# One more empty part on the attention chain's way out, and shared-expert pieces left out beside every fourth part of the last chain

## The chip, the cores and the metric

The kernel runs on one NeuronCore of a Trainium2 chip (trn2). The metric is the device time of one execution in microseconds: 706.55 us is the median of three timed runs before the change (703.7 to 708.07). The engines are named as in the profile: PE (TensorE matmul), PEld (its weight loads), DVE (VectorE), ACT (ScalarE), POOL (GpSimd) and SP (SyncE, which issues most DMAs).

## The reference: what is computed

Two transformer layers over 4 sequences of 512 tokens with 128 features, each sublayer followed by a residual and a layernorm:

```
x = LN(x + banded_attention(x))      # 16 heads of 8, each token sees 64 to either side
x = LN(x + moe0(x))                  # shared GEGLU expert (256 wide) + top 2 of 12 GEGLU experts (384 wide)
x = LN(x + ssm(x))                   # state-space mixer, 4 heads of 64, sequence of 64 states
x = LN(x + moe1(x))                  # top 2 of 8 experts (512 wide), each with its own layernorm
```

The change touches the attention and the first MoE. There, with `g` the weights of the two chosen experts:

```
ys = geglu(x @ Ws1 + bs1) @ Ws2 + bs2                        # every token
yr = sum over chosen e of g[e] * (geglu(x @ We1[e] + be1[e]) @ We2[e] + be2[e])
x  = LN(x + ys + yr)
```

## The kernel before

**Attention.** `attention` runs a software pipeline over g = -5 to 33. A batch has 8 steps (four blocks of 128 keys, two halves of heads). Each turn of the loop writes, in this order: `attention_exp` of step g (scores `pse`, L808; exponentials on ACT, L812; band mask on POOL, L816), a slot; `attention_max_end` and `attention_max` of steps further ahead (band and scores `psc`, L771 and L778; row maxima on DVE, L784; `pmax`, L791; the update of `q`, L794), a slot; `attention_values` of step g - 2 (`pc`, L831, then at a batch's end the copy `sum`, L838), a slot. All of it is traced under `as_written`, which keeps each engine's instructions in the order of the program (only the scatters of one run may change places among themselves).

**Chains.** What follows a batch's attention is a chain of parts, a generator; each slot (`advance(1)`) runs one part. A chain starts at the last slot of g = 8b + 9, so that three run inside the loop and the fourth has one part there. In order the parts are, for one batch:

- `attention_out`: (1) POOL adds the bias to x (L844), DVE turns the sums and inverts (L849, L851); (2) DVE spreads the inverses (`wide`, L854), turns them (L856) and scales both sums (L859); (3) nothing; (4) the output projection on PE (`po`, L865); (5) DVE adds it to x (L870) and takes statistics (L323, L324); `layernorm`: (6) square root on ACT (L304); (7) reciprocal and offset on DVE (L306, L314); (8) ACT normalises (L317).
- `moe0_shared`: (9) nothing; (10) transposes and their copy (`tp_xt`, L295, L298); (11) nothing; (12) the router (`pl`, L958); `gates`: (13) the first maximum (L340 to L354); (14) the second, and a tanh on ACT (L368); (15) gate weights (L375 to L381); then `moe0_dense` of this batch is put on the list `later`; `route`: (16) `rh` on DVE (L419) and two POOL writes (L422, L425); (17) ranks on PE (`prank`, L430 to L439); (18) DVE works out the rows `put` (L445 to L459); (19) to (22) two scatters each on POOL (L472); for the last batch (23) `route_end`, which makes the table of tiles on DVE (L485 to L516).

**Shared experts.** `moe0_dense` has six pieces: (1) the gates' transposes `tp_gt` on PE and a memset on POOL (L977, L979); (2) the copy `gt` on ACT (L981), two matmuls `pg_s` (L986) and their GELU `ge_s` (L990); (3) two matmuls `pa_s` (L995); (4) `act_s` on DVE (L998); (5) the projection `pys` (L1005, L1007); (6) the add `y` on DVE (L1012). None runs inside the loop.

**Tail.** After the loop `attention` returns `tail()`, which gives out the fourth chain's remaining parts and puts one piece of `later` behind each. `tiles` then works through the 43 expert tiles (PE `pxs_a` L560, `pg` and `pa` L1028, `py_a` L580; loads on SP, L547 and L548; scatter on POOL). It cannot write the first load before the table of tiles exists (`while "rows" not in r: next(beside)`), so the tail runs up to `route_end` first; what is left of it is written beside the tiles, at a budget of 1.0 us a tile against the cost that each piece yields.

PSUM has one pool of six banks that `psc`, `pse`, `po`, `pmax`, `tp_xt`, `pl`, `pg_s`, `pa_s`, `pys` and the tiles take in turn: a bank is free again when its reader has read it.

Of the kernel before, what the change touches and what calls it, by code (L numbers as in the profile page):

```python
# [39 lines left out]
class Kernel:  # L40
# [57 lines left out]
    def behind(self, x, y):  # L98

        order = mybir.DependencyInfo(mybir.DependencyClass.NoSync, mybir.DependencyReason.DATA)  # L100
        self.tc.add_manual_dep(x.ins, y.ins.name, order, reason="as written")
# [738 lines left out]
    def attention_out(self, b, s):  # L840

        nc = self.nc
        xb = s["x"][..., :D]
        nc.gpsimd.tensor_tensor(xb, xb, self.bo[:, None, :].to_broadcast([P, NT, D]), ALU.add)  # L844

        inv = self.sm.tile([P, 16, 4], F32, tag="inv", name=f"inv{b}")
        for cp in range(2):
            turned = self.ctx.tile([P, 16, 32], F32, tag="turned", name=f"turned{b}_{cp}")
            nc.vector.transpose(turned.rearrange("p k r -> p (k r)"), s["sum", cp])  # L849
            at = 16 - 16 * cp  # L850
            nc.vector.reciprocal(inv[:, :, 2 * cp : 2 * cp + 2], turned[:, :, at : at + 16 : HD0])  # L851
        yield 2.1
        wide = self.ctx.tile([P, 16, 4, HD0], F32, tag="turned", name=f"wide{b}")
        nc.vector.tensor_copy(wide, inv[:, :, :, None].to_broadcast([P, 16, 4, HD0]))  # L854
        scale = self.ctx.tile([P, T], F32, tag="turned", name=f"scale{b}")
        nc.vector.transpose(scale, wide.rearrange("p k c d -> p (k c d)"))  # L856
        for cp in range(2):
            x = s["sum", cp]
            nc.vector.tensor_tensor(x, x, scale, ALU.mult)  # L859
        yield 2.5  # L860
        yield 0.0
        po = self.bank(f"po{b}")
        for i in range(NT):
            for cp in range(2):
                nc.tensor.matmul(  # L865
                    po[:, i * P : (i + 1) * P], lhsT=s["sum", cp][:, i * P : (i + 1) * P],
                    rhs=self.wo2[:, cp, :], start=cp == 0, stop=cp == 1,
                )
        yield 1.5
        nc.vector.tensor_tensor(xb, po.rearrange("p (i d) -> p i d", i=NT), xb, ALU.add)  # L870
        mv = self.small([P, NT, 2], "mv", 6)
        for i in range(NT):
            self.stats(xb[:, i, :], mv[:, i, :])
        yield 2.6
        yield from self.layernorm([xb[:, i, :] for i in range(NT)], mv)
        return s["x"]

    def attention(self, x, behind):

        self.attention_consts()
        steps = 2 * NT
        ahead, lag = 5, 2
        state = [{} for _ in range(NB)]
        chains, self.later = [], []

        def chain(b):
            y = yield from self.attention_out(b, state[b])  # L890
            yield from behind(b, y)

        def advance(n):
            for c in list(chains):
                for _ in range(n):
                    if next(c, None) is None:
                        chains.remove(c)
                        break

        for _ in self.attention_qk(0, x[0], state[0]):  # L900
            pass
        for g in range(-ahead, NB * steps + lag):
            b, u = divmod(g, steps)
            if 0 <= b < NB:
                self.attention_exp(b, u, state[b])
            if g == 0:
                chains.append(self.ssm_consts())
            advance(1)
            b, u = divmod(g + ahead - 1, steps)
            if u % 2 and 0 <= b < NB:  # L910
                self.attention_max_end(b, u // 2, state[b])
            b, u = divmod(g + ahead, steps)
            if b < NB:
                self.attention_max(b, u, state[b])
            advance(1)
            b, u = divmod(g - lag, steps)
            if 0 <= b < NB:
                self.attention_values(b, u, state[b])
                if u == steps - 1:
                    chains.append(chain(b))  # L920
            if g == -ahead:
                self.attention_weights()
            b, u = divmod(g + ahead + 4, steps)
            if 0 < b < NB and u < 3:
                if u == 0:
                    state[b]["qk"] = self.attention_qk(b, x[b], state[b])
                next(state[b]["qk"])
            b, u = divmod(g + steps - 3, steps)
            if u == 0 and b < NB:
                self.attention_v(b, state[b])  # L930
            advance(1)

        def tail():

            parts = (part for c in chains for part in c)
            for part in parts:
                yield part
                while self.later:
                    if next(self.later[0], None) is not None:
                        break  # L940
                    self.later.pop(0)
            for c in self.later:
                yield from c

        return tail()


# [856 lines left out]
```

## Time and profile before

| | us |
|---|---|
| median of three timed runs | 706.55 |
| their range | 703.7 to 708.07 |
| the profiled execution, device time | 697.46 |
| its span, first to last instruction | 695.8 |
| its busy time: PE | 511.5 |
| PEld | 374.2 |
| DVE | 417.3 |
| POOL | 357.3 |
| ACT | 313.4 |

The profile was taken of one execution with a mean granted TensorE clock of 0.83. A timeline line gives start, duration, engine, source line, operation, output and inputs, shape, count, and in brackets how long the engine had been idle before and what released it. In lines of busy time by stretches, the pairs after the comma are busy us and (number of instructions) of PE, PEld, DVE, ACT and POOL; the last three numbers are the granted clock, the DMA engines' share and GB/s. Line numbers are those of the kernel before; after the change those below L860 are one higher, and those below L937 four.

### The profile page before, as it was taken

The page shows a single profiled execution, that of the slowest core. Times are in us where ns is not written, and L with a number is a line of the kernel's source. Part 1 is how long each engine was busy: PE and PEld are TensorE (multiplying, and loading weights), DVE is VectorE, ACT ScalarE, POOL GpSimd, SP SyncE. Part 2 cuts the span into 40 slices and gives each one's busy share as a digit, 9 for nine tenths or more (in the row PEclk, how much of TensorE's full clock was granted, in tenths as well). Part 3 has the DMA queues.
Part 4 walks back from the last instruction along what each step waited for, and adds up shares of the span by engine and source line. Part 5 has one row for each costly group of instructions (what it writes and reads, how often), then busy time and mean ns, then how long its engine had stood idle before and what let it go on. Part 6 is the DMA issues. An engine that isn't in the chain of part 4 may idle for free. (4 is left out here: it accounts for less than half of the span.)

```text
span 695.8 us, 13449 instructions
## 1 busy us (share of the span) xinstructions
PE 511.5 (74%) x4264; PEld 374.2 (54%) x4264; DVE 417.3 (60%) x1412; ACT 313.4 (45%) x816; POOL 357.3 (51%) x509
## 2 busy tenths in 40 slices
PE   6899788779977894999994474853675669899700
PEld 2344354254544553999994342622464469888700
DVE  5565656666734361466663359799784526777845
ACT  2154544443461511355552666934323317566525
POOL 8354323823747032355553217378773646888830
PEclk9899989979978695899998566977575559999955
DMA  6999999993000004488884402212110135666442
GB/s 171 244 162 164 165 165 162 166 163 51 32 2 32 0 16 152 126 254 251 239 255 148 144 0 78 76 48 76 46 48 19 44 112 168 167 181 170 121 130 61
DMA packets 93936, 83.63 MB, mean 120 GB/s; under 512 B 8869, under 2 KB 78650, under 8 KB 93866
## 3 DMA queue, kind: packets, MB, share of 16 engines
q1 hardware_dynamic: 88554, 71.85, 47.0%
q0 software_dynamic: 5312, 10.92, 5.2%
q8 instruction: 35, 0.57, 0.4%
q14 instruction: 35, 0.29, 0.1%
HBM read 50.54 MB, written 32.20 MB: 119 GB/s over the span
## 5 line engine op out<-in xcount | busy, mean ns | idle before, releaser
L816 POOL TENSOR_SCALAR_AFFINE_SELECT pt<-pt 128x1024 f32<-128x1024 f32 (+1 forms) x64 | 61.6, 987 | 95.4 <-ACT pt L812 89.1
L784 DVE TENSOR_REDUCE maxima<-psc 128x2 f32<-128x384 f32 x128 | 62.4, 549 | 45.3 <-PE psc L778 45.3
L812 ACT ACTIVATE pt<-pse 128x384 f32<-128x384 f32 (+1 forms) x128 | 59.2, 550 | 64.0 <-PE pse L808 64.0
L472 POOL DMA_INDIRECT ys_a<-io_a,at_a x43 | 42.1, 979 | 50.5 <-DVE at_a L571 37.9
L1037 DVE SCALAR_TENSOR_TENSOR act<-pa,bias_a,ge 128x128 f32<-128x128 f32 x129 | 37.4, 345 | 50.1 <-ACT ge L1036 29.1
L1631 ACT ACTIVATE hid<-ph,bias_b 128x128 f32<-128x128 f32 x156 | 44.6, 369 | 23.7 <-PE ph L1628 21.2
L771 PE MATMUL psc<-band,ident_bf 128*64 128x384 bf16 (+1 forms) x192 | 39.3, 351 | 12.6 <-ACT pt L812 7.5
L1036 ACT ACTIVATE ge<-pg,bias_a 128x128 f32<-128x128 f32 x129 | 38.1, 366 | 21.4 <-DVE at_a L571 17.7
L472 POOL DMA_INDIRECT table_a<-x,put x32 | 31.9, 996 | 24.6 <-issue 14.8
L1628 PE MATMUL ph<-io_b,wt_b 128*128 128x128 f32 x312 | 43.2, 283 | 0.0
L472 POOL DMA_INDIRECT ys_b<-io_b,at_b x39 | 39.1, 1002 | 7.4 <-issue 5.5
L808 PE MATMUL pse<-q,k 32*128 32x256 f32 (+1 forms) x512 | 41.1, 394 | 1.8 <-DVE q L794 1.8
L472 POOL DMA_INDIRECT table_b<-r,put x32 | 32.1, 1003 | 19.6 <-issue 7.9
L580 PE MATMUL py_b<-down,hid 128*128 x312 | 41.8, 277 | 0.3
L1628 PEld LDWEIGHTS ph<-io_b,wt_b 128*128 128x128 f32 x312 | 39.5, 199 | 0.0
L580 PEld LDWEIGHTS py_b<-down,hid 128*128 128x128 f32 x312 | 38.1, 192 | 1.2 <-issue 0.7
L1028 PE MATMUL pg<-io_a,wt_a 128*128 128x128 f32 x258 | 37.2, 282 | 0.0
L808 PEld LDWEIGHTS pse<-q,k 32*128 32x128 f32 x512 | 29.1, 198 | 15.0 <-issue 6.8
L1028 PE MATMUL pa<-io_a,wt_a 128*128 128x128 f32 x258 | 37.1, 282 | 0.0
L580 PE MATMUL py_a<-down,act 128*128 x258 | 35.8, 276 | 0.0
L831 PE MATMUL pc<-pt,v 128*32 128x256 f32 (+1 forms) x512 | 34.1, 390 | 0.6 <-POOL pt L816 0.6
L1028 PEld LDWEIGHTS pa<-io_a,wt_a 128*128 128x128 f32 x258 | 33.6, 199 | 0.0
(342 smaller groups left out, 1222.0 us busy)
## 6 DMA issues: line engine op xcount, KB each, us to landing
wt_a<-in_We_dram SPq DMA_DIRECT2D x43, 384.0 KB
table_a<-zero SPq DMA_DIRECT2D x12, 1040.0 KB
wt_b<-in_w_dram SPq DMA_DIRECT2D x39, 256.0 KB
table_b<-zero SPq DMA_DIRECT2D x8, 1040.0 KB
dbc<-rows SPq DMA_DIRECT2D x8, 512.0 KB
io_a<-table_a SPq DMA_DIRECT2D x43, 65.0 KB
io_b<-table_b SPq DMA_DIRECT2D x39, 65.0 KB
down<-in_We_dram SPq DMA_DIRECT2D x12, 192.0 KB
```

The lines of the kernel that those rows point to most:

```text
L472: put = self.nc.gpsimd.indirect_dma_start(out=out, out_offset=bass.IndirectOffsetOnAxis(ap=at, axis=0), in_=x, in_offset=None)
L580: nc.tensor.matmul(py[:, :D], lhsT=hidden[:, c * P : (c + 1) * P], rhs=flat[:, bass.ds(r["reg"][t, 2] + c * D, D)], start=c == 0, stop=c = ...
L771: nc.tensor.matmul(pp[part], lhsT=self.ident_bf[:, part], rhs=self.band[:, None, off : off + w].to_broadcast([P, 2, w]), start=True, stop= ...
L784: nc.vector.tensor_reduce(self.maxima[b % 2][:, j, at : at + 2], pp, AX.X, ALU.max)
L808: nc.tensor.matmul(pp[:, c], lhsT=s["k"][strip, 2 * cp + c, m * P : (m + 1) * P], rhs=s["q"][strip, c, lo:hi], start=True, stop=True, skip ...
L812: nc.scalar.activation(pt[:, 2 * i : 2 * i + 2, :w], pp, AF.Exp)
L816: nc.gpsimd.affine_select(out=x, in_=x, compare_op=ALU.is_ge, fill=0.0, base=HALF if m == 0 and sign > 0 else 0, pattern=[[0, 2 * G], [sig ...
L1028: nc.tensor.matmul(p[:, c * P : (c + 1) * P], lhsT=wt[:, at : at + P], rhs=xt, start=True, stop=True,)
L1036: nc.scalar.activation(ge[:, cb], pg[:, cb], AF.Gelu, bias=bias[:, 3 + c : 4 + c])
L1037: nc.vector.scalar_tensor_tensor(act[:, cb], pa[:, cb], bias[:, c : c + 1], ge[:, cb], ALU.add, ALU.mult)
L1628: nc.tensor.matmul(ph[:, cb], lhsT=s["wt"][:, cb], rhs=s["xt"], start=True, stop=True)
L1631: nc.scalar.activation(hid[:, cb], ph[:, cb], AF.Gelu, bias=s["bias"][:, c : c + 1])
```

## The change

In `attention_out` a second part without work stands between the scaling of the sums and the output projection, so that every later part of each chain comes one slot later. In `tail` the parts are counted from 0, and behind parts 3, 7, 11, 15 and 19 (and so on) no piece of the shared experts is written.

```diff
@@ attention_out
             x = s["sum", cp]
             nc.vector.tensor_tensor(x, x, scale, ALU.mult)
         yield 2.5
+        yield 0.0
         yield 0.0
         po = self.bank(f"po{b}")
@@ tail
             parts = (part for c in chains for part in c)
-            for part in parts:
+            for n, part in enumerate(parts):
                 yield part
+
+                if n % 4 == 3:
+                    continue
                 while self.later:
                     if next(self.later[0], None) is not None:
                         break
```

## Prediction

> **What bounds the kernel now.** The chain of work that ended last is traced back only to 485 us of the span, behind both edits, so I read the stages from busy time by stretches (columns: PE, weight loads, DVE, ACT, POOL busy us with counts, granted TensorE clock, DMA share, GB/s), then from each engine's timeline.
>
> ```profile
> 81.90:133.40 51.50, 43.26 (x488) 22.62 (x488) 31.90 (x93) 24.45 (x50) 21.77 (x24) 0.93 1.19 164
> ...
> 213.50:266.60 53.10, 40.18 (x172) 25.17 (x172) 22.76 (x71) 14.67 (x24) 20.52 (x28) 0.82 0.06 20
> ...
> 285.50:373.30 87.80, 87.74 (x786) 87.51 (x783) 57.01 (x253) 46.98 (x163) 48.17 (x81) 1.00 0.77 231
> ```
>
> First row: one batch's round of the attention loop. PE leads (43 of 51.5 us) and loses 8 us to waits. Second: the tail, where no engine is full; one dependent chain sets it. Third: the expert tiles, where PE has no gap at all: each matmul added there is paid in full. What follows waits for the tiles' results, so a shift up to 373 us reaches the end.
>
> PE's timeline shows where it stops:
>
> ```profile
> 86.57 3.81 PE L865 MATMUL po<-wo,sum 128*128 128x128 f32 x16 [2.53 <-DVE sum L859]
> ...
> 99.34 0.84 PE L771 MATMUL psc<-band,ident_bf 128*64 128x384 bf16 x4 [1.56 <-ACT pt L812]
> ...
> 273.40 0.79 PE L1005 MATMUL pys<-be,gt 13*128 13x128 f32 x2
> 275.16 1.45 PE L1007 MATMUL pys<-w_Ws,act_s 128*128 128x128 f32 x4 [0.97 <-DVE act_s L998]
> ```
>
> The output projection waits 2.53, 4.96 and 0.93 us in the three rounds inside the loop and then runs at the low clock (3.81, 3.87, 2.34 us). Just behind, PE waits for exponentials; ACT's timeline says why:
>
> ```profile
> 93.64 1.28 ACT L304 ACT_TABLE_LOAD   x1
> 94.93 0.30 ACT L304 ACTIVATE rstd<-mv,eps 128x4 f32<-128x4 f32 x1
> 97.40 1.28 ACT L812 ACT_TABLE_LOAD   x1 [2.17 <-PE pse L808]
> 98.69 2.06 ACT L812 ACTIVATE pt<-pse 128x512 f32<-128x512 f32 x4
> ```
>
> The layernorm's square root costs two table loads, and the next exponentials stand behind it. On DVE:
>
> ```profile
> 94.37 1.95 DVE L784 TENSOR_REDUCE maxima<-psc 128x2 f32<-128x384 f32 x4 [0.97 <-PE psc L778]
> ...
> 135.48 3.36 DVE L854 COPY wide<-inv 128x512 f32<-128x512 f32 x1
> ...
> 247.92 0.69 DVE L1012 TENSOR_TENSOR y<-pys,x 128x512 f32<-128x512 f32 x1 [2.57 <-PE pys L1007]
> ```
>
> Every step's four row maxima hold DVE for 1.95 us; what is written behind them waits.
>
> **The change, part by part.** No instruction is added or removed. The empty part moves each later part of a chain by one slot of the written order (after the exponentials, after the maxima, after the values). The skip takes pieces n = 3, 7, 11, 15, 19 out of the tail: 21 pieces ran before the routing table's end, 17 will.
>
> *First round in the loop.* The projection now stands behind the next step's scores (pse). Half of these have free banks and run at 84.0; the other half needs banks that the maxima release only after the scaled sums on DVE (86.94 + 2 x 0.49 = 87.9). The projection starts near 88.4, still at the low clock until about 90.4, and ends near 91.3: pmax starts at 91.3 against 91.41 before, and the maxima are 0.8 us earlier. So the filled wait brings under 1 us. But the add and the statistics (2.4 us) were ahead of the maxima and are now behind them: 93.55 + 1.95 + 2.4 = 97.9. The square root, queued ahead of the next exponentials on ACT, then needs 1.28 + 0.30, and the exponentials' table 1.28: they start at 100.8, not 98.69. **+2.1 us**; PE waits for their banks. Moving the turn (tp_xt) and its copy behind the scores is neutral. Next, the second half of the gates comes behind the maxima instead of ahead: the tanh on ACT waits until 118.4 (before 112.96), and that step's exponentials, queued behind it, start 3.5 us later instead of 2.1. PE's step ends **+3.3 us** in all (2 to 4.5).
>
> *Second round.* The same +3.3, less what happens to the copy at 135.48: 3.36 us against 0.43 in the third round, because three POOL instructions run one after another until 138.56. With the scatters one slot later (they are DMA issues; in the third round the same copy ran beside them at 0.43), the copy should fall beside scatters: -2.9. Then the two scalings (1.29 us) meet POOL's add and selects. The Trainium skill (SBUF — State Buffer, section "Who interferes with whom") says that a DVE instruction with two SBUF inputs contends with a GpSimd one that reads SBUF. The trace has it: a 128x48 product took 1.09 us beside a select, 0.21 without. By the copy's row alone the round is +0.4; by this rule the stall moves to the scalings and nearly all of it stays, +3.0. I take the middle, **+1.8** (0.3 to 3.3).
>
> *Third round*, without further maxima: the scores' wait for q (1.81) goes, but the root waits for statistics at 195.0 and holds the exponentials 2.0 us; normalising, turn and router follow, the router's matmuls about 2 us late; part is made up. The place write on POOL is now behind the last select (about 214.4), so the eight scatters start near 215.1 instead of 214.16: **+1.0** (-0.5 to 2.7). They are queued ahead of the last chain's add on POOL (DVE's x waited 6.5 us for it), so all of it passes on.
>
> *Tail.* Up to the router PE does the same work in another order: no change. Behind it, the first gates no longer wait for act_s (1.6), and the y add that stood between the gates' halves (2.57 + 0.69) moves to just ahead of rh, which the ranks need. It waits there for pys, which waits for act_s, now behind the first gates. With the router's end at 244.6: gates 1.66, act_s 1.6, pys from 247.9; 4.3 us at full clock (243.59 to 247.92), or over 7 at half (275.16 to 282.2). At full clock y ends at 252.9 and the last scatter near 265.6, which is 0.4 better than before once the +1.0 is taken off. The clock decides, and it was low in the same matmuls before:
>
> ```profile
> 230.40:233.80 3.40, 3.40 (x11) 2.50 (x12) 0.34 (x2) 2.16 (x6) 0.00 (x0) 0.50 0.00 0
> 233.80:237.20 3.40, 3.40 (x14) 2.64 (x15) 0.52 (x1) 0.00 (x0) 0.00 (x0) 0.50 0.00 0
> ```
>
> The skill (TensorE: Matmul & The Clock Gate, Part 1) lets the clock fall after an idle window of some 3.4 us and rise after as long a busy one. By that rule PE's new 1.8 us of waiting would leave it full: tail -0.4. But the rows show 0.50 through seven busy microseconds of pys, and a gap of 1.56 us at 97.8 was followed by 0.54 over 100.2 to 103.5. I go by the rows: full for half a window, then low, pys takes some 5.9 us and the tail is **+1.2** (-1.0 to +3.5). The table's end on DVE (5.2 us) comes behind act_s of batch 2 and ends about with the scatters: 0. It was hidden under the scatters before (262.06 against 265.04); that cover shrinks to about nothing.
>
> *Tiles.* Before, batch 3's pys stood behind tile 0: 273.40 to 282.0, 8.6 us at low clock, then tile 1; tile 0's down ended at 285.45. Now tp_gt and pg follow tile 0 (1.06 + 3.42 cold), then tile 1 and the down (1.66 + 0.83 warm to 3.0 + 1.6 cold): 280.4 to 282.5. Later pa (1.88) and pys (4.65, warm) come on top. They were hidden in the tail (pg and pa under the scatters after 256); here PE has no gap, so they cost. Sum 286.9 to 289.0 against 285.45: **+2.5** (1.5 to 3.5). ACT's two ge_s (1.27), DVE's act_s (1.4) and two y adds (0.69 each) fit into a tile's 2.12 us with little stall. SP's loads run three tiles ahead and stay there.
>
> Sum: 3.3 + 1.8 + 1.0 + 1.2 + 2.5 = **+9.8 us**. The profiled execution took 697.46 us (span 695.8), 9.1 below the median of the timed runs; it would become about 707.3. On the median of 706.55: **716.3 us**.
>
> **Rivals.** (1) *It evens out.* The waits on ACT are pipelined effects, and a round that meets them elsewhere may lose 0.5 each; tail 0, tiles +1.5: +3.0, 709.6 us. For: PE had small waits for pt in every step (7.5 us in 19 places) that a shift can absorb. Against: a late square root lands on no slack, ACT's wait is on PE's path one step later.
> (2) *Faster: the projection's wait really goes.* The waits are 2.53 + 4.96 + 0.93 = 8.4 us, and at full clock (about 1.9) the three projections give back another 4.3: 12.7 us; with tail and tiles +3.7 this is -9.0, 697.5 us. It decides from about 11 us recovered. Against: half of the scores put into the gap need banks that DVE frees after the sums.
> (3) *The change does little in the loop, the tail decides alone:* +3.7, 710.3 us; it falls in with (1).
>
> **How the numbers follow.** About 1% (7 us) is what a measurement of this kernel can tell from no change. My forecast 0.55, nearly all of it slower by over 1%; (1) and (3) 0.30, within 1%; (2) 0.15, faster. The range of 702 to 722 leaves out the far half of (2) and the case in which all upper bounds come together (17.5 us, 724). Slower cases alone: 713.7 to 722.
>
> **What would show it.** Right: the square root after the first round starts near 98, not 93.6, with exponentials after it near 101; the tanh behind the maxima; rh behind a y add that waited for pys; tile 1's matmuls before 280 and pys among the tiles at about 4.7 us. Wrong: projections at under 2 us without a wait and rounds of under 51 us; a copy of 0.43 and no stall in the scalings after it; a first tile load earlier than 266.6.

## The result and the profile after

The changed kernel took **716.71 us** (median of four runs, 714.87 to 717.49), the kernel before 706.88 beside it (703.7 to 708.07): a ratio of 1.0153, 95% interval 1.0117 to 1.019. That is slower by over 1%, and 0.4 us from the predicted 716.3. The sum was right; two of its terms were not, and they cancelled. In what follows a ratio compares only each kernel's fast executions (those within 1.5% of its fastest), while a median is of all of them; by that rule the profile b_again is of a slow execution, at an equal mean clock (0.832 against 0.830).

The profiled execution of after took 717.49 us (span 715.8). That of before, shown above, was an unusually quick one (697.46). A second profile of the same kernel (label b_again) took 711.58 us, span 709.9. After is compared with this second one in what follows, unless the text says otherwise; the two spans differ by 5.9 us.

The stages first, cut at the first turn of each batch's sums, the first tile load and the last tile's matmuls. Columns as before: PE, weight loads, DVE, ACT, POOL busy us (count), granted clock, DMA share, GB/s. After:

```profile
80.30:140.50 60.20, 49.30 (x488) 25.18 (x488) 31.98 (x92) 24.18 (x49) 24.23 (x27) 0.85 1.23 154
140.50:193.80 53.30, 46.78 (x475) 24.50 (x473) 30.37 (x91) 18.96 (x39) 18.59 (x21) 0.81 0.72 91
193.80:232.70 38.90, 31.44 (x259) 18.54 (x262) 19.07 (x53) 17.53 (x35) 18.77 (x20) 0.69 0.03 10
232.70:286.40 53.70, 39.38 (x160) 25.21 (x160) 22.09 (x70) 12.69 (x20) 19.91 (x29) 0.75 0.06 20
286.40:391.40 105.00, 101.32 (x853) 97.72 (x853) 59.99 (x260) 51.16 (x175) 48.31 (x83) 0.97 0.73 216
```

The second profile of before:

```profile
80.40:133.70 53.30, 43.33 (x488) 22.68 (x488) 31.79 (x92) 23.77 (x47) 21.55 (x24) 0.93 1.19 150
133.70:183.40 49.70, 40.92 (x476) 22.46 (x473) 32.91 (x90) 19.60 (x40) 22.12 (x25) 0.90 0.95 130
183.40:220.30 36.90, 26.65 (x269) 15.29 (x269) 20.65 (x53) 17.86 (x35) 18.86 (x21) 0.77 0.03 9
220.30:276.10 55.80, 42.37 (x167) 26.27 (x156) 22.75 (x72) 14.30 (x23) 19.65 (x27) 0.79 0.06 19
276.10:382.80 106.70, 101.16 (x841) 98.78 (x841) 59.56 (x258) 49.43 (x172) 48.27 (x82) 0.93 0.72 212
```

The three rounds of the loop are 6.9, 3.6 and 2.0 us longer, 12.5 together. The tail is 2.1 shorter, the tiles 1.7, what follows them 2.7. Now read the first pair after the comma. In the loop PE does the same matmuls (488, 475 against 476, 259 against 269, some records missing), but is busy 127.5 us with them against 110.9: **16.6 us more busy, 4.1 us less idle**. The same work takes longer, and the granted clock fell from 0.93, 0.90, 0.77 to 0.85, 0.81, 0.69. In most short stretches (those shown further on, for example) the clock is either full or half. If it were only ever one of the two, these means would make 62 us at half clock in the three rounds after and 34 before (an estimate from the rows above): 28 us more, which lose 14 us of work, most of the 16.6.

Against the first profile of before, whose rounds took 132.2 us with PE busy for 107.1 and idle for 25.1, the rounds are 20.2 us longer, all of it busy time. Much of what parts the two profiles of before is a stall on ACT that comes and goes (last section). After has it too, so the second is the closer match.

PE's timeline of after, in the first round (start, duration, then what ran; in brackets the idle time ahead of it):

```profile
82.34 1.14 PE L808 MATMUL pse<-q,k 32*128 32x256 f32 x8
85.91 2.53 PE L808 MATMUL pse<-q,k 32*128 32x256 f32 x8 [2.43 <-DVE maxima L784]
88.37 3.76 PE L866 MATMUL po<-wo,sum 128*128 128x128 f32 x16
```

PE's waits over the three rounds (total us, times, longest), after and then the second profile of before:

```profile
PE psc L771 <- ACT pt L812: 11.9, 15, 3.5
PE pse L808 <- DVE maxima L784: 4.6, 3, 2.4
```

```profile
PE psc L771 <- ACT pt L812: 12.3, 15, 4.3
PE po L865 <- DVE sum L859: 6.4, 2, 3.9
```

The projection no longer waits for the scaled sums. The scores written ahead of it wait instead: half of them have free banks, the other half needs banks that the row maxima release, and those stand behind the sums on DVE. PE's waits for exponentials (`pt`) are no longer than before.

The square root on ACT, after:

```profile
89.12 1.28 ACT L304 ACT_TABLE_LOAD   x1
98.16 0.30 ACT L304 ACTIVATE rstd<-mv,eps 128x4 f32<-128x4 f32 x1 [7.76 <-DVE mv L324]
98.48 1.28 ACT L812 ACT_TABLE_LOAD   x1
99.77 2.06 ACT L812 ACTIVATE pt<-pse 128x512 f32<-128x512 f32 x4
...
117.85 0.20 ACT L368 ACTIVATE ge<-ge 128x4 f32<-128x4 f32 x1 [3.57 <-DVE ge L362]
```

It starts at 98.16 and holds the exponentials to 99.77; the tanh stands at 117.85. DVE, after, in the second and third round and in the tail:

```profile
142.59 0.92 DVE L854 COPY wide<-inv 128x512 f32<-128x512 f32 x1
144.28 1.29 DVE L859 TENSOR_TENSOR sum<-sum,scale 128x512 f32<-128x512 f32 x2
...
200.43 4.48 DVE L859 TENSOR_TENSOR sum<-sum,scale 128x512 f32<-128x512 f32 x2
...
271.68 0.69 DVE L1016 TENSOR_TENSOR y<-pys,x 128x512 f32<-128x512 f32 x1 [3.97 <-PE pys L1011]
272.29 0.20 DVE L419 TENSOR_TENSOR rh<-e_gh 128x48 bf16<-128x48 f32 x1
```

In the tail `rh` stands behind a y add that waited 3.97 us for `pys`, as forecast, and `pys` ran at low clock there (third number from the right):

```profile
265.80:269.20 3.40, 3.40 (x13) 2.61 (x13) 1.50 (x10) 0.21 (x1) 0.00 (x0) 0.54 0.02 5
269.20:272.60 3.40, 2.50 (x11) 1.76 (x11) 0.92 (x4) 0.00 (x0) 0.00 (x0) 0.50 0.00 0
```

### The profile page after: what moved, and what is told of

Its sections match the earlier page's. It is cut to its first block, busy times and chain, and to the rows that moved or that the text cites. A ratio compares the mean times of both kernels' runs of the same rounds, so it can differ in the third digit from the quotient of the medians.

```text
span 715.8 us, 13447 instructions
## 1 busy us (share of the span) xinstructions
PE 523.4 (73%) x4264; PEld 377.0 (53%) x4264; DVE 416.2 (58%) x1412; ACT 312.6 (44%) x816; POOL 357.1 (50%) x509
## 5 line engine op out<-in xcount | busy, mean ns | idle before, releaser
L1041 DVE SCALAR_TENSOR_TENSOR act<-pa,bias_a,ge 128x128 f32<-128x128 f32 x129 | 37.3, 344 | 45.5 <-ACT ge L1040 23.4
L771 PE MATMUL psc<-band,ident_bf 128*64 128x384 bf16 (+1 forms) x192 | 41.5, 365 | 21.1 <-ACT pt L812 13.5
L808 PE MATMUL pse<-q,k 32*128 32x256 f32 (+1 forms) x512 | 51.9, 411 | 6.1 <-DVE maxima L784 4.6
L808 PEld LDWEIGHTS pse<-q,k 32*128 32x128 f32 x512 | 35.6, 206 | 23.3 <-issue 11.1
L1040 ACT ACTIVATE ge<-pg,bias_a 128x128 f32<-128x128 f32 x129 | 37.9, 365 | 20.6 <-DVE at_a L571 16.6
L831 PE MATMUL pc<-pt,v 128*32 128x256 f32 (+1 forms) x512 | 36.4, 411 | 0.6 <-POOL pt L816 0.6
L771 PEld LDWEIGHTS <-ident_bf 128*64 128x64 bf16 (+1 forms) x192 | 14.1, 113 | 42.7 <-issue 35.9
L1032 PE MATMUL pg<-io_a,wt_a 128*128 128x128 f32 x258 | 36.5, 279 | 0.0
L1032 PE MATMUL pa<-io_a,wt_a 128*128 128x128 f32 x258 | 36.5, 278 | 0.0
```

The source lines that it names most:

```text
L771: nc.tensor.matmul(pp[part], lhsT=self.ident_bf[:, part], rhs=self.band[:, None, off : off + w].to_broadcast([P, 2, w]), start=True, stop= ...
L808: nc.tensor.matmul(pp[:, c], lhsT=s["k"][strip, 2 * cp + c, m * P : (m + 1) * P], rhs=s["q"][strip, c, lo:hi], start=True, stop=True, skip ...
L1032: nc.tensor.matmul(p[:, c * P : (c + 1) * P], lhsT=wt[:, at : at + P], rhs=xt, start=True, stop=True,)
L1040: nc.scalar.activation(ge[:, cb], pg[:, cb], AF.Gelu, bias=bias[:, 3 + c : 4 + c])
L1041: nc.vector.scalar_tensor_tensor(act[:, cb], pa[:, cb], bias[:, c : c + 1], ge[:, cb], ALU.add, ALU.mult)
```

## The experiments

Three theories were open. **Loop**: the parts' new places among scores, maxima and exponentials cost it all. **Way out**: the tail's and tiles' new order costs a part of it. **Even**: nothing but chance between executions, since one kernel's profiles lay 14 us apart.

**Both kernels again, and each edit alone.** Median of before beside these four: 706.45 us. Line numbers are each run's own.

> The kernel before, profiled a second time. The first profiled execution (697.46 us) lies 9 us below the median of its timed runs. If something that comes and goes lies in single executions (in the trace after: ACT idle 5.5 and 6.8 us ahead of the copies of the sums with nothing to wait for), this profile shows such stalls too and ends near 706; if the first profile is typical, it ends near 697 and shows none.

> The kernel after, profiled a second time. If ACT's idle stretches belong to single executions, the rounds of the attention loop (from one batch's first turn of the sums to the next) are shorter here than the 60.2, 53.3 and 38.9 us of the first profile of after, by about 4 and 6 in the first two or elsewhere, and stalls appear in other places. If they are made by the change, they stand in the same places again.

b_again: 707.62 us, ratio 0.9966 (0.9933 to 0.9998). a_again: 721.64, ratio 1.0236 (1.0196 to 1.0276). "Even" falls: the change costs about 15 us here, and 10 in the first comparison. The rounds of a_again (61.2, 53.3 and 38.9 us) repeat those of after, with ACT's stalls in the same places.

```diff
@@ e_part: attention_out alone
         yield 2.5
+        yield 0.0
         yield 0.0
```

> Only the empty part, no skip. By my steps the loop costs +6.1, the tail about +2 (the router then stands behind one more projection of the shared experts, the y add is ahead of the gates instead of between them), the tiles 0: 714.6 us in all (+8). By the rival that it evens out in the loop, +1 to +3. By the rival that the wait of the projection goes, -10 to -12, 696 us.

721.42 us, ratio 1.0232 (1.0196 to 1.0268): the empty part alone costs what the whole change costs, about twice what I had given it. Its three rounds take 152.5 us, those of after 152.4.

```diff
@@ e_skip: tail alone
-            for part in parts:
+            for n, part in enumerate(parts):
                 yield part
+                if n % 4 == 3:
+                    continue
```

> Only the skip, no empty part. By my steps the loop is 0, the tail -1 to +1 (the router stands ahead of two matmuls of the shared experts, but the place computation stands behind a y add), the tiles +2 to +3: 708 to 710 us. By the rival in which tail and tiles decide all of it, the whole +10 shows here (717).

711.10 us, ratio 1.0036 (1.0 to 1.0071). Alone, the skip leaves the loop as it was (138.8 us against 139.9), and moves work from the tail (52.4 us against 55.8) into the tiles (115.0 against 106.7). Beside the empty part it adds nothing that shows.

**Which place in the loop.** One empty part at a time was put further back along the chain, so that the parts ahead of it keep their old places. Before beside these four: 707.03 us, on another chip than the four above.

```diff
@@ x_stats: between the projection and the add to x with its statistics
+        yield 0.0
@@ x_root: between the statistics and the square root (layernorm)
+        yield 0.0
@@ x_gates: behind the gates, ahead of route
+        yield 0.0
@@ x_step: attention_out, the whole chain one step (three slots) later
         yield 2.5
+        yield 0.0
+        yield 0.0
+        yield 0.0
         yield 0.0
```

> One empty part, no skip, but behind the output projection instead of ahead of it: the projection keeps its old slot, wait and clock; add and statistics come behind the maxima, the root late, the gates late. If the late root and the late tanh on ACT make the loss, nearly all of the +15 that the empty part alone took is here (717 to 722). If it is the projection's place (scores cut in two by the banks, then both at the low clock), little is left: 707 to 712.

715.07 us, 1.0113 (1.0075 to 1.0151): between the two expectations.

> The empty part between statistics and root: projection, add and statistics in their old slots, so the root has its statistics in time and only comes one slot later; the second half of the gates still comes behind the maxima. By the theory of the late root the first loss of each round (+2 and the low clock behind it) goes and the tanh's (+1 to +2 a round) stays: 709 to 713. If the gates make the larger part, 715 and more.

707.62 us, 1.0018 (0.9998 to 1.0037): less than either expectation.

> The empty part between gates and route: all of the above in the old slots, only ranks, rows and scatters one slot later. By my steps nothing is left in the loop; scatters a little later, tail +1 to +2 (its pieces are as in the run with the empty part alone behind this point): 706 to 709. If any added slot costs (for instance because all pieces of the tail stand differently), 712 and more.

708.73 us, 0.9991 (0.9963 to 1.0018).

> Three empty parts instead of one, no skip: every part behind them keeps the slot that it had before (statistics ahead of the maxima, gates ahead of the maxima), one whole step later; only the projection's wait for the scaled sums should go. If the slot decides, this costs nothing in the loop and the projection's waits (2.5, 4 to 5, 1 us) and its low clock go: 698 to 706. If later parts cost by being late, as the chain of the next batch or the scatters would, it is slower than the run with one part: over 721.

705.58 us, 0.9985 (0.9961 to 1.0009).

Read with the rounds' stretches:

| kernel | three rounds, us | PE busy | PE idle | at half clock (estimate, as above) |
|---|---|---|---|---|
| before, first profile (no stalls on ACT) | 132.2 | 107.1 | 25.1 | 27 |
| before, second profile | 139.9 | 110.9 | 29.0 | 34 |
| x_gates | 140.9 | 117.5 | 23.4 | 44 |
| x_root | 139.8 | 115.0 | 24.8 | 37 |
| x_stats | 146.2 | 118.6 | 27.6 | 44 |
| e_part | 152.5 | 126.4 | 26.1 | 61 |
| after | 152.4 | 127.5 | 24.9 | 62 |
| x_step (short stalls only) | 132.9 | 111.5 | 21.4 | 29 |

Each row is one execution. The total of before, x_gates and x_root, which share ACT's stalls, agrees within 1.1 us, but how it falls into busy and idle time scatters by some 6 us. Two steps carry the loss, and in both the intervals of the ratios lie apart (0.9998 to 1.0037, 1.0075 to 1.0151, 1.0196 to 1.0268). From x_root to x_stats (+6.4 us) the add and the statistics move from ahead of a step's maxima to behind them. ACT in x_root, then in x_stats:

```profile
92.17 1.28 ACT L304 ACT_TABLE_LOAD   x1
93.47 0.30 ACT L304 ACTIVATE rstd<-mv,eps 128x4 f32<-128x4 f32 x1
```

```profile
94.33 1.28 ACT L304 ACT_TABLE_LOAD   x1
99.87 0.30 ACT L304 ACTIVATE rstd<-mv,eps 128x4 f32<-128x4 f32 x1 [4.26 <-DVE mv L324]
100.18 1.28 ACT L812 ACT_TABLE_LOAD   x1
```

The root stands at the same place of ACT's order in both; only in x_stats must it wait, and the exponentials wait behind it. From x_stats to e_part (+6.3 us) the projection moves behind the scores: PE's idle time falls by 1.5 us, its busy time grows by 7.8, and 17 us more are at half clock. Filling the wait trades little idle time for much slow work; the fall in idle time is within the scatter, but the three profiles with the projection in that place (e_part, after, a_again: 126.4 to 128.8 us busy) lie above all others (118.9 at most). The later gates and tanh (x_gates to x_root) show no cost over the rounds, though ACT waits 3.58 us for them.

x_step moves the chain by all three slots of a step: every part stands again where it stood before among maxima and exponentials, only one step later. PE's two first projections there run without a wait and fast:

```profile
97.81 1.95 PE L868 MATMUL po<-wo,sum 128*128 128x128 f32 x16
148.42 1.95 PE L868 MATMUL po<-wo,sum 128*128 128x128 f32 x16
```

The rounds take 132.9 us, as in the first profile of before (132.2), which like this one lacks the long stalls on ACT, although the delay is three times that of the change. **Which slot, not how late, decides.** The 7 us to the second profile of before are no gain of the slots that is shown: that profile has the stalls. The last chain is a step late too: from its first turn to the first load it takes 68.4 us, against 55.8 in the second profile of before, and the kernel as a whole is no faster.

**Loop and way out apart.** A number of empty parts for the three chains inside the loop, and another for the last chain. Before beside these four: 699.8 us (a third chip).

```diff
@@ attention_out
         yield 2.5
         yield 0.0
+        for _ in range(X if b < NB - 1 else Y):
+            yield 0.0
```

v_tail is X = 0, Y = 1 with the skip; v_loop3 X = 3, Y = 0 without it; v_loop2 X = 2, Y = 0 without; v_both X = 3, Y = 1 with the skip.

> The change in the tail alone: the empty part for the last batch only, and the skip; the loop as before. By the prediction's steps tail +1.2 and tiles +2.5: 710 to 711. By the traces of after against the second trace of before (tail -1.8, tiles -1.7 to +0.8): 703 to 707.

698.39 us, ratio 1.0004 (0.9971 to 1.0037). The tail and the tiles of the change, with the loop of before, cost nothing that shows (-2.0 to +2.6 us by the interval); "way out" falls.

> Three empty parts for the first three batches only, the tail as before. In the run with three for all, the projections ran in 1.95 us without a wait and the three rounds took 133 us against 140 in the second trace of before, but the tail was 12 us longer. If both are what they seem, this takes 698 to 702; if the tail's length there came from the loop (scatters later on POOL), 705 to 708.

699.43 us, ratio 1.0031 (1.0004 to 1.0058). The loop of x_step with the tail of before brings nothing over before here. None of these four profiles has the stalls on ACT, and the rounds are alike: 132.4 us in v_tail, whose loop is before's, and 133.3 here.

> Two empty parts for the first three batches only: the projection stands behind the maxima's scores, add and statistics in the slot behind the values, the root behind the next exponentials on ACT instead of ahead of them. If the harm of one part is the root ahead of exponentials with its statistics late, two parts do no harm: 700 to 706. If it is any shift against the maxima, 712 and more.

716.0 us, ratio 1.0298 (1.0252 to 1.0343): the theory that only the root with late statistics does harm falls. Two slots are as bad as one. The rounds take 147.9 us, 15.5 more than v_tail's, 12.2 of them PE's busy time (118.9 against 106.7). ACT and PE in the first of them:

```profile
101.85 1.28 ACT L304 ACT_TABLE_LOAD   x1
103.15 0.30 ACT L304 ACTIVATE rstd<-mv,eps 128x4 f32<-128x4 f32 x1
104.37 1.65 ACT L317 ACTIVATE x<-x,off_mean,rstd 128x128 f32<-128x128 f32 x4 [0.92 <-DVE off_mean L314]
106.03 1.28 ACT L812 ACT_TABLE_LOAD   x1
```

```profile
107.97 0.32 PE L771 MATMUL psc<-band,ident_bf 128*128 128x384 bf16 x1 [3.25 <-ACT pt L812]
```

Here the root no longer waits for its statistics, but root and normalising stand together between two steps' exponentials. Both table loads, the root and the normalising (1.28 + 0.30 + 0.92 + 1.65 + 1.28) hold the next exponentials, and PE waits 3.25 us for their banks. In v_loop3 the normalising comes behind the next exponentials and the same wait is 1.47. And all of the gates is behind one maximum, so that the tanh makes ACT wait 5.65 us. This is read from one trace; the two were not tried apart.

> Three empty parts for the first three batches, one for the last, and the skip: the tail of the change with a loop that keeps its slots. If the change's tail and tiles are worth -2 to -3, this is the fastest: 696 to 701. If they cost what the prediction said (+3.7), 702 to 706.

697.48 us, ratio 1.0044 (1.0012 to 1.0077), while its median is 2.3 us below before's: no difference that can be told.

## Why the prediction was right, point by point

**The order of events held, the last link did not.** The root was forecast near 98 and ran at 98.16, the exponentials at 100.8 and ran at 99.77, the tanh at 118.4 and ran at 117.85. This is closer than it deserves, since the round began 1.6 us earlier here. Counted from the round's first turn (81.93 in the profile that the forecast used, 80.30 here), the root was forecast at 16.0 and came at 17.9, the exponentials at 18.9 and 19.5, the tanh at 36.5 and 37.6. The root is late because the projection ends late (below). The exponentials lost less, since the table for the root had been loaded at 89.12, in the wait. The second half of the scores waits for banks, `rh` waits behind y and `pys`, and `route_end` ends with the scatters (284.4 and 284.8). But "PE waits for their banks" is not where the loss stands: PE's waits for exponentials are 11.9 us after and 12.3 in the second profile of before, and the loss is in PE's busy time, most of it at half clock by the estimate above.

Rival 1 (it evens out) falls with e_part, rival 3 (the tail decides alone) with v_tail. Rival 2 (faster, the wait really goes) needed projections of about 1.9 us without a wait; they took 3.76, 3.78 and 3.73 inside the loop. Its own argument against, the scores' banks, is what the trace shows.

**The loop was mis-sized: +6.1 forecast, +12.5 measured against the second profile (+20.2 against the first, which the forecast was worked from).** The term that failed is "the filled wait brings under 1 us" with the projection "at the low clock until about 90.4". By that working it ends 9.4 us behind the first turn. It ended 11.8 behind it; before, 8.5. And moving the projection alone (x_stats to e_part) costs 6.3 us over the rounds, where the forecast put a small gain and counted nothing. PE's gap is as long as before (2.43 us against 2.52), but it ends a little later. Stretches of 3.4 us, after and then the second profile of before:

```profile
85.30:88.70 3.40, 2.79 (x9) 1.99 (x10) 1.95 (x5) 0.68 (x2) 0.00 (x0) 0.50 1.15 153
88.70:92.10 3.40, 3.40 (x17) 3.27 (x16) 0.00 (x0) 1.69 (x2) 2.13 (x2) 0.52 1.39 142
92.10:95.50 3.40, 3.40 (x50) 1.96 (x48) 2.26 (x6) 0.00 (x0) 0.00 (x0) 1.00 1.14 163
...
98.90:102.30 3.40, 2.41 (x22) 0.77 (x22) 0.24 (x2) 3.39 (x7) 0.34 (x1) 0.50 1.26 156
102.30:105.70 3.40, 3.40 (x35) 1.49 (x28) 1.95 (x4) 1.05 (x3) 1.80 (x2) 0.51 1.28 154
...
119.20:122.60 3.40, 3.36 (x37) 1.23 (x40) 1.66 (x5) 0.38 (x1) 2.13 (x4) 0.51 1.29 159
```

```profile
85.40:88.80 3.40, 3.35 (x15) 3.06 (x14) 1.93 (x5) 0.00 (x0) 0.00 (x0) 0.51 1.24 146
88.80:92.20 3.40, 2.94 (x34) 1.59 (x41) 2.74 (x11) 2.12 (x5) 0.00 (x0) 0.99 1.21 155
...
99.00:102.40 3.40, 3.40 (x36) 1.31 (x20) 1.95 (x4) 1.78 (x5) 2.13 (x2) 0.51 1.25 150
```

In both, the clock falls to 0.5 at about 85.4. Before, PE fills the low stretch (3.35 of 3.40 us) and the next one is at full speed. After, PE restarts at 85.91, leaves that stretch short (2.79), and a second one follows at half speed, full of work (3.40 us). The Trainium skill (TensorE: Matmul & The Clock Gate, Part 1) lets the clock rise after a busy window of this length; these rows agree with that; those of `pys` do not (last section). The same happens behind the late exponentials: 2.41 us busy, and the low clock stays for a second stretch, where before one full stretch was enough. A third low place stands behind the late tanh. So after has five low stretches in this round where the second profile of before has two. As an estimate, each costs 1.7 us of work (half of 3.4): three more make 5.1 of the 6.0 us by which PE's busy time in the round grew. That these edges set the size is argued from the rows; no run moved an edge alone. What is shown is the step from x_stats to e_part, in their times and in PE's busy time.

The late root was sized about right: 2.1, 2.1 and 2.0 us forecast for the three rounds, 6.4 measured over them (x_root to x_stats). The late tanh, forecast at another 1.2 in each of the first two rounds, shows no cost over the rounds of x_root. A low stretch does follow it there in the first round (clock 0.50 from 114.6 to 116.3), but one behind the exponentials, which x_gates has (0.50 from 101.0 to 102.7), is missing: where the low stretches fall differs from one kernel and execution to the next.

**Second round, the copy against the scalings.** The copy took 0.92 us (3.52 in the second profile of before), but not beside the scatters: the last of them ended at 139.93, and the copy, from 142.59, ran beside a select (141.08 to 143.21). The scalings, from 144.28, came when POOL had finished, so their 1.29 says nothing on two SBUF inputs. In the third round the forecast's rule fits, with POOL's add (from 200.49) and selects (from 201.62) beside the scalings: 4.48 us, against 2.21 in the second profile of before, also beside selects, and 1.29 in the first. The forecast had put the collision in the second round and named none in the third.

**Tail and tiles were given +3.7 and cost nothing** (v_tail 1.0004; after against the second profile -3.8). In the tail y waits for a slow `pys`, as written, and it is worth little: v_tail's tail takes 53.6 us, v_loop3's, written as before, 52.9. In the tiles the added matmuls run fast. PE in v_tail, then in v_loop3, on the same chip, first loads at 268.48 and 268.43:

```profile
275.28 0.97 PE L982 MATMUL tp_gt<-ident,e_g 128*12 128x128 f32 x4
276.08 1.88 PE L991 MATMUL pg_s<-xt,w_Ws 128*128 128x512 f32 x4
277.80 0.27 PE L560 MATMUL pxs_a<-ident,io_a 128*128 128x128 f32 x1
277.91 0.83 PE L1033 MATMUL pg<-io_a,wt_a 128*128 128x128 f32 x6
```

```profile
284.14 0.42 PE L560 MATMUL pxs_a<-ident,io_a 128*128 128x128 f32 x1
284.35 1.49 PE L1030 MATMUL pg<-io_a,wt_a 128*128 128x128 f32 x6
```

I had put `pg_s` at 3.42 us cold; it took 1.88, and tile 1 begins 6.3 us earlier. With `pys` gone from between the first tiles, tile 1 runs at full clock (0.83 us for six matmuls against 1.49), and the stretch takes 105.4 us with 853 matmuls against 107.0 with 841. So what came on top was paid by the clock. The forecast +3.7 lies outside what v_tail allows (-2.0 to +2.6 us); that the true cost is below nothing is not shown.

In sum, against the second profile: 6.4 us too little for the loop, 7.5 too much for tail and tiles. The stages of the two profiles differ by only 5.9 us, since the second profile of before lies itself 4.0 above that kernel's median (711.58 against 707.62); the medians differ by 9.8, as forecast, and by some 15 in the second set. That the total came within 0.4 us is luck: two errors of opposite sign, and a first comparison that came out 5 us lower than the second.

## What to carry to other kernels

Where two chains share engines in a written order, ask of each moved operation which long instruction it now stands behind (row maxima, exponentials), not how much later it comes: in this loop one slot cost 12 us or more, two slots 15, three none. Filling a wait on TensorE with work that needs the same release only moved the wait here, and a gap that ended a little later went with another stretch at half clock; price a stretch by PE's busy time for the same number of matmuls, not by its idle time alone. A total that agrees proves none of its terms: only a run with each part alone does.

## What the runs showed of the hardware, unlooked for

One kernel's executions differ by several us in the loop. In the second profile of before ACT stood idle ahead of the second copy of `sum` in a batch, with a releaser outside the core's own engines; in the first profile the same instruction waited for its matmuls alone. The second, then the first:

```profile
187.00 0.58 ACT L838 COPY sum<-pc 128x512 f32<-128x512 f32 x1 [6.32 <-remote]
```

```profile
181.95 0.59 ACT L838 COPY sum<-pc 128x512 f32<-128x512 f32 x1 [1.71 <-PE pc L831]
```

In the second profile PE then waited 4.26 us for the exponentials behind that copy. After shows 6.75 us there. Such stalls, of 4 to 7 us at the second copies of the second and third batch, stand in both profiles of after, in b_again, e_part, e_skip, x_gates, x_root and x_stats; the first profile of before, x_step (3.34 us at most) and the four profiles on the third chip lack them. So they are not made by the change, and rounds with them should be compared only with rounds that have them. Of the 14.1 us between the two spans of before, 7.7 lie in the loop. The cause is open; no run tried it.

`pys` in the tail and among the first tiles ran through full stretches without the clock rising (3.40 of 3.40 us busy at 0.54 from 265.8, and 0.50 in the next, above; in the second profile of before 3.40 of 3.40 at 0.58 from 286.3 and again at 0.50 from 289.7), while a filled stretch in the loop was enough. What sets these apart is open too.
